# Last batch of a fused cross-attention kernel: value columns ahead of residual additions, copies ahead of the root, two scores moved, small operations later

## The chip, the cores and the metric

The kernel runs on one core of a Trainium2 chip. The time is that of one execution on the device, in microseconds (us). Five engines matter: TensorE (PE in the profile) for matrix products, VectorE (DVE), ScalarE (ACT) and GpSimd (POOL) for elementwise work, and SyncE (SP), whose queue issues the DMAs.

## The reference

Eight batches of 112 queries with 320 channels attend, with 20 heads of 16 channels, to 371 text tokens; four more tokens are image prompts. Beside the usual attention, the text probabilities also weight the raw 512-wide text embeddings; that weighted sum is normalised and compared with the normalised prompts, and the comparison is added to the prompts' own scores. Everything is float32.

```python
q = heads(hidden_states @ W_q)
k_t, v_t = heads(text_ehs @ W_k), heads(text_ehs @ W_v)
probs_t = softmax(einsum('bhsd,bhtd->bhst', q, k_t) * attn_scale)
text_out = einsum('bhst,bhtd->bhsd', probs_t, v_t)
attn_scores = einsum('bhsd,bhnd->bhsn', q, k_ip) * attn_scale      # four prompts
qsem = l2norm(einsum('bhst,bte->bhse', probs_t, text_ehs))
sem = einsum('bhsd,bnd->bhsn', qsem, l2norm(ip_ehs))
probs_ip = softmax(attn_scores + SEM_SCALE * sem) * spatial_mask
out = (text_out + einsum('bhsn,bhnd->bhsd', probs_ip, v_ip)) @ W_out + b_out + residual
```

## The kernel before

The batches 0 to 7 are worked through in turn, each in five groups g = 0 to 4 of four heads. The norm of the weighted embeddings is had without forming them: with p the unnormalised probabilities of a head and G the Gram matrix of the text tokens, p G is formed, and its dot product with p is the squared norm. So each head has, in `u`, the columns of G with 21 more columns beside them: four for the prompts, one of ones and sixteen for the head's values. One chain of products per head gives all of it in one bank `ps_qd` of 112 x 392.

A head passes through these helpers:

- `scores` (L652, TensorE): q k into a score bank `ps_s`, 375 columns with the prompts.
- `maxima` (L674, VectorE) and `exponentials` (L688 and L690, ScalarE): negated row maximum `nmx`, p = exp, and a copy `ipl` of the four prompt scores, which is the last reader of the score bank. `probabilities` is both, and `sent` (L695, SyncE) a DMA that deals p into `xg`.
- `turned` (L704, VectorE): the transposes of `xg` into `xgT`, in two halves.
- `multiplied` (L723, TensorE): twelve steps j, in each of which the four heads of the group run side by side in row groups of 32, from 392 columns at j = 0 down to 40. The helper yields after every step, and other work is put between the steps.
- `placed` (L621, GpSimd): copies the group's value columns from `vr` into `u`, in three chunks. The products of the group need them, and a chunk can be overwritten only when the group before has read it.
- `reduced` (L769, VectorE, `junk`): the dot product with p of one head. `shared` does the same for some heads with other engines: copies out of the bank on ScalarE (L753 value sums `pvs`, L754), a product on GpSimd (L758), a sum on ScalarE (L762). `value_sums` (L736) copies `pvs` for the heads that `shared` doesn't take.

`finish` then handles all heads of a batch: `z2`, `zr`, the division `attn` (L811, GpSimd), `rn` (L824), its root (L828, ScalarE, table Sqrt), a preload of the Exp table (L829), the reciprocal of `rn` and four more operations on `fu` (L834 to L840, VectorE), `ex` (L844, ScalarE), `sx`, `rx`, `w` (L848 to L852, VectorE), and then `ps_wT`, `wT`, `ps_a`, `aT`, `ps_o` (L858 to L894). It is a generator; each call of `run` or `next` issues one piece of it. `with_bias` (L783, GpSimd) adds bias to the residual. `last_heads` does the same for the last four heads of the last batch.

The order of instructions on every engine is written out by hand: the program text is the order. The steady loop `steps` covers batches 0 to 6. The last batch, b = 7, is a loop of its own at the end, in which the `finish` of batch 6 (`before`), the tail of batch 5 (its `ps_o` and output) and that of batch 7 itself (`first`, 16 heads, and `last`, 4 heads) are interleaved with the groups. There the scores of group 3 and group 4 are made in groups 0 and 1. Of the eight banks of 512 columns, four are `ps_qd`, two `ps_sc` and two `ps_mm`. `bank(..., spare=True)` takes a `ps_sc` bank, `bank(...)` a `ps_mm` bank. The scores of group 4 use the `ps_qd` banks, since groups 1 and 3 of the last batch accumulate in the other four.

Of the kernel before, what the change touches and what calls it, by code (L numbers as in the profile page):

```python
# [9 lines left out]
AF = mybir.ActivationFunctionType  # L10
# [10 lines left out]
def kernel(  # L21
# [63 lines left out]
    def bank(name, spare=False):  # L85

        if spare:
            return ps_sc.tile([P, 512], F32, tag="sc", name=name)
        return ps_mm.tile([P, 512], F32, tag="mm", name=name)
# [602 lines left out]
    def sent(b, g, a):  # L692

        xg = x_ring[(b * NG + g) % NX]
        nc.sync.dma_start(xg[a * RG : a * RG + S // QN, :, :TT], st[b]["p", g][:, a, :])  # L695
# [69 lines left out]
    def reduced(b, g, a0=0, a1=GROUP):  # L765
        s = st[b]
        for a, (h, ps) in list(enumerate(zip(groups[g], s["qd", g])))[a0:a1]:
            junk = small.tile([S, TT], F32, tag="junk", name=f"junk_{b}_{h}", bufs=1)
            nc.vector.tensor_tensor_reduce(  # L769
                out=junk,  # L770
                in0=ps[:S, :TT],
                in1=s["p", g][:, a, :],
                scale=1.0,
                scalar=0.0,
                op0=ALU.mult,
                op1=ALU.add,
                accum_out=s["ss"][:, h : h + 1],
            )
        if a1 == GROUP:
            del s["p", g]  # L780
# [5 lines left out]
    def finish(b, heads=(0, H), bd=None):  # L786
# [20 lines left out]
        ah = attn[:, :C].rearrange("p (h d) -> p h d", d=D)[:, part]  # L807

        def divided():
            nc.vector.reciprocal(zr, z)  # L810
            eng.tensor_tensor(  # L811
                ah, pvs[:, :, NIP + 1 :], zr.unsqueeze(2).to_broadcast([S, n, D]), ALU.mult
            )
# [4 lines left out]
                with_bias(b)  # L818
        nc.vector.scalar_tensor_tensor(z2, z, EPS * EPS, z, ALU.mult, ALU.mult)
        if bd is not None:  # L820
            divided()
            yield

        nc.vector.tensor_tensor(rn, s["ss"][:, part], z2, ALU.max)  # L824
        if bd is None:
            yield
# [1 line left out]
        nc.scalar.activation(rn, rn, AF.Sqrt)  # L828
        nc.scalar.preload_act_table(AF.Exp)  # L829
        if bd is None:  # L830
            divided()
        yield

# [217 lines left out]
    def drain(*gens):  # L1051
        for gen in gens:
            for _ in gen:
                pass
# [5 lines left out]
    def run(key, make, pieces=1):  # L1060

        if key not in gens:
            gens[key] = make()
        for _ in range(pieces):
            next(gens[key], None)
# [141 lines left out]
    for n, (b, g) in enumerate(steps[:-NG]):  # L1207
        if n == len(steps) - NG - 3:
            ctx.enter_context(
                tc.manual_schedule(  # L1210
                    engines=engines | {mybir.EngineType.Activation, mybir.EngineType.Pool}
                )
            )
        now, more, then = ahead(n)
        for c, a in now:
            scores(*c, a)
            probabilities(*c, a)
        for j, _ in enumerate(multiplied(b, g)):
            if j == 0:
                for c, a in more:  # L1220
                    scores(*c, a, ps=bank(f"ps_s_{c[0]}_{c[1]}_{a}"))
                    probabilities(*c, a, hold=True)
            if j == 5:
                for c, a in then:
                    scores(*c, a)
                held = more + [(c, a) for c, a in then if c == steps[n + LEAD + 1]]
                for c, a in then:
                    probabilities(*c, a, hold=(c, a) in held)
                drain(turn)
                for c, a in held:  # L1230
                    sent(*c, a)
            if j == 2:
                if g == 0:
                    gram_banks(b + 1)
                turn = turned(*steps[n + 1], 2 * QN)
                next(turn)
                if n == 0:
                    run(("c", LEAD), None)
                if 1 <= g <= 3:
                    gram_to_groups(b + 1, {1: (0,), 2: (1,), 3: (3,)}[g], parts=halves[g == 2])  # L1240
                for c, i in x_loads.get((b, g), ())[:1]:
                    load_x_blocks(c, i)

                if g in (1, 2) and b > 0:
                    run(("f", b - 1), None)
        value_sums(b, g)
        if g == 2 and b > 0:
            run(("f", b - 1), None)
        if n == len(steps) - NG - 1:
            sums = shared(b, g, GROUP // 2)  # L1250
            next(sums)
            reduced(b, g, 2)
        else:
            reduced(b, g)
        placed(*steps[n + 1])
        if g == 0 and b > 1:
            run(("f", b - 2), None)
        load_rest(n)
        if n == 0:
            load_embed(nc.sync, wkip_sb, w_k_ip)  # L1260
            load_embed(nc.sync, wvip_sb, w_v_ip)
        if g in ctx_blocks and b < B - 3:
            load_ctx_blocks(b + 3, ctx_blocks[g])
        for c, i in x_loads.get((b, g), ())[1:]:
            load_x_blocks(c, i)
        if g == 1:
            gram_to_groups(b + 1, (0,), parts=halves[1])
            gram_to_groups(b + 1, (1,), parts=halves[0])
        elif g == 2:
            gram_to_groups(b + 1, (2,))  # L1270
        elif g == 3:
            gram_to_groups(b + 1, (3,), parts=halves[1])
        if g in (2, 3) and b == 0:
            run(("pp",), None)
        if (b, g) == (B - 2, 0):
            prompt_values_by_head()
        if (b, g) == (B - 2, 1):
            bd = load_prompt_values_by_head()
        if (b, g) == (B - 2, 3):
            own_channels(bd)  # L1280
        if g == 0 and b > 0:
            prompt_values(b - 1)
        between(b, g)
        if n == NG - 1:
            drain(prompt_logits(b))
# [1 line left out]

    b = B - 1
    before = ("f", b - 1)
    next(sums)  # L1290
    run(("q", b), None)

    for g in range(NG):
        for j, _ in enumerate(multiplied(b, g)):
            if g == 0 and j in (0, 3):
                some = (2, 3) if j == 0 else (0, 1)
                for a in some:
                    scores(b, NG - 2, a, ps=bank(f"ps_s_{b}_{NG - 2}_{a}", spare=a > 1))
                for a in some:
                    probabilities(b, NG - 2, a, hold=True)  # L1300
                if j == 0:
                    turn = turned(b, 1)
                    next(turn)
                else:
                    drain(turn, sums)
                    for a in (2, 3, 0, 1):
                        sent(b, NG - 2, a)
            if g == 1 and j in (5, 6):
                for a in ((3, 2), (1, 0))[j - 5]:
                    ps = ps_qd.tile([P, 512], F32, tag="qd", name=f"ps_s_{b}_{NG - 1}_{a}")  # L1310
                    scores(b, NG - 1, a, ps=ps)
                    probabilities(b, NG - 1, a, hold=True)
                if j == 6:
                    drain(turn)
                    for a in (3, 2, 1, 0):
                        sent(b, NG - 1, a)
                    nc.scalar.preload_act_table(AF.Sqrt)
                    run(before, None)
            if (g, j) in ((2, QN), (2, 2 * QN), (3, QN)):
                run(before, None)  # L1320
            if g > 1 and j == 2 * QN:
                drain(sums)
            if 0 < g < NG - 1 and j in (QN - 1, 2 * QN - 1):
                placed(b, g + 1, (j // QN,))
        if g == NG - 1:
            break
        n = (3, 3, 2, 1)[g]
        earlier, sums = sums, shared(b, g, n)
        next(sums)
        reduced(b, g, n)  # L1330
        if g < NG - 2:
            value_sums(b, g, n)
            turn = turned(b, g + 2)
            if g == 0:
                next(turn)
            else:
                drain(turn, earlier)
            placed(b, g + 1, range(NT) if g == 0 else (NT - 1,))
            next(sums)
        if g == 0:  # L1340
            run(before, lambda: finish(b - 1, bd=bd[:, 0]))
            with_bias(b - 1)
            with_bias(b)
            run(("f", b - 2), None)
        if g == 2:
            nc.scalar.preload_act_table(AF.Sqrt)
        if g == 3:
            value_sums(b, g, 1)
            placed(b, g + 1, (NT - 1,))
            drain(sums)  # L1350
            first = finish(b, (0, FULL * HC), bd=bd[:, 1])
            for _ in range(4):
                next(first)
    late = projected_prompts(bd[:, 1])
    last = last_heads(b)
    run(before, None)
# [68 lines left out]
```

## Time and profile before

| | |
|---|---|
| median of three runs (lowest, highest) | 408.5 us (407.34, 408.51) |
| profiled execution, its own time | 407.31 us |
| span of its instructions | 405.6 us |
| granted TensorE clock | 0.999 |
| TensorE busy | 398.2 us, 98% of the span |
| VectorE, ScalarE, GpSimd busy | 341.1, 190.6, 118.2 us |

The own time of the profiled execution lies 1.7 us above its span. It is as short as the lowest of the three runs. In the rows of a timeline the columns are start and length in us, engine, line, operation, the tile written and the tiles read, shapes, and the number of instructions that the row merges; in brackets stands the idle time of the engine ahead of it and what ended it. The last batch takes from about 363 us to the end.

### The profile page before, as it was taken

Reading aid. Unit: us, or ns where it says so; the run is one execution under the profiler, and the core shown is the slowest. Engines: PE = TensorE matmul, PEld = TensorE weight load, DVE = VectorE, ACT = ScalarE, POOL = GpSimd, SP = SyncE. Lnnn points to the kernel's source line nnn. Section 1 sums busy time; section 2 is a strip of 40 time slices with the busy share of each in tenths; the row PEclk is TensorE's granted clock in tenths of the full one; section 3 lists DMA queues with packets and bytes.
Section 4 is the critical chain, followed back from the end, with each engine's and each line's share of the span. In section 5 each row is a group of like instructions: output and inputs, shape, how many; then the busy total and the mean of one; then the engine's idle time right before and its main releaser. Section 6 shows DMA issues by size and latency. Waiting matters only on the chain.

```text
span 405.6 us, 13896 instructions
## 1 busy us (share of the span) xinstructions
PE 398.2 (98%) x5442; PEld 313.9 (77%) x5442; DVE 341.1 (84%) x730; ACT 190.6 (47%) x664; POOL 118.2 (29%) x282
## 2 busy tenths in 40 slices
PE   9999999999999999999999999999999999999796
PEld 8658787987788877787777877788778887788793
DVE  5678797888998899788998989789898878886985
ACT  3553343545335634446334453445434463455883
POOL 6611110111342206022061212512143220715640
PEclk9999999999999999999999999999999999999999
DMA  6984665656645555465555555454445355544400
GB/s 214 215 186 115 218 165 146 155 153 183 151 126 135 159 146 141 106 152 168 138 146 145 149 145 137 118 141 149 121 118 142 99 172 140 134 113 127 116 3 30
DMA packets 46433, 56.94 MB, mean 140 GB/s; under 512 B 9405, under 2 KB 40961, under 8 KB 46368
## 3 DMA queue, kind: packets, MB, share of 16 engines
q1 hardware_dynamic: 46328, 55.99, 52.2%
q8 instruction: 43, 0.70, 0.7%
q14 instruction: 22, 0.18, 0.1%
q10 hardware_dynamic: 40, 0.07, 0.1%
HBM read 15.88 MB, written 1.39 MB: 43 GB/s over the span
## 4 chain that ended last, share of the span: by engine, by line
PE 95%; POOL 1%; issue 1%; ACT 1%; DVE 1%; POOLq 0%; DVEq 0%
PE ps_qd L723 40%; PE ps_k L541 16%; PE ps_s L652 11%; PE ps_v L541 10%; PE ps_g L507 7%; PE ps_q L359 4%; PE ps_o L943 3%; PE ps_g L463 1%; POOL shared L758 1%; PE ps_w L442 1%; PE ps_o L894 1%; PE ps_c L426 0%; PE ps_a L931 0%; PE ps_ipkv L298 0%; DVE nmx L674 0%
## 5 line engine op out<-in xcount | busy, mean ns | idle before, releaser
L723 PE MATMUL ps_qd<-u,xgT 32*112 32x168 f32 (+11 forms) x3840 | 216.6, 350 | 2.8 <-POOL u L621 2.8
L723 PEld LDWEIGHTS ps_qd<-u,xgT 32*112 32x112 f32 x3840 | 185.7, 172 | 27.3 <-POOL u L621 3.0
L688 ACT ACTIVATE p<-ps_s,nmx 112x371 f32<-112x371 f32 x156 | 84.3, 578 | 96.0 <-DVE nmx L674 89.5
L704 DVE STREAM_TRANSPOSE xgT<-xg 128x512 f32<-128x512 f32 (+2 forms) x79 | 126.0, 1598 | 0.7 <-DMA xr_sb<-in_x_dram 0.4
L674 DVE TENSOR_REDUCE nmx<-ps_s 112x1 f32<-112x371 f32 x160 | 78.8, 537 | 26.9 <-PE ps_s L652 22.7
L769 DVE CUSTOM_DVE_ANT_0 junk<-ps_qd,p 112x371 f32<-112x371 f32 x146 | 79.2, 542 | 19.5 <-ACT pvs L736 3.9
L621 POOL COPY u<-vr 128x64 f32<-128x64 f32 x120 | 26.4, 239 | 140.5 <-PE ps_qd L723 96.5
L652 PE MATMUL ps_s<-kT,qm 32*112 32x375 f32 (+1 forms) x320 | 64.7, 495 | 0.0
L541 PE MATMUL ps_k<-ctxT,wk_sb 128*128 128x371 f32 x192 | 64.6, 484 | 0.0
L541 PEld LDWEIGHTS ps_k<-ctxT,wk_sb 128*128 128x128 f32 x192 | 35.1, 190 | 20.3 <-ACT vT L563 0.5
L541 PE MATMUL ps_v<-ctxT,wv_sb 128*128 128x371 f32 x128 | 42.4, 482 | 0.0
L541 PEld LDWEIGHTS ps_v<-ctxT,wv_sb 128*128 128x128 f32 x128 | 23.7, 190 | 14.5 <-issue 0.5
L652 PEld LDWEIGHTS ps_s<-kT,qm 32*112 32x112 f32 x320 | 25.0, 171 | 12.6 <-issue 10.8
L507 PE MATMUL ps_g<-ctxT 128*32 128x375 f32 (+11 forms) x672 | 30.4, 333 | 0.0
L507 PEld LDWEIGHTS ps_g<-ctxT 128*32 128x32 f32 x672 | 27.7, 110 | 2.0
L556 ACT COPY kT<-ps_k 128x371 f32<-128x371 f32 x24 | 11.2, 468 | 37.9 <-PE ps_k L541 37.9
L690 ACT COPY ipl<-ps_s 112x4 f32<-112x4 f32 x140 | 23.0, 164 | 0.0
L414 DVE STREAM_TRANSPOSE ctxT<-ct 128x512 f32<-128x512 f32 x21 | 22.8, 1095 | 0.0
L918 POOL TENSOR_TENSOR wv<-vip,w 112x1280 f32<-112x1280 f32 x6 | 14.8, 2464 | 26.5 <-DVE w L852 26.5
L479 ACT ACTIVATE ug<-ps_g 128x375 f32<-128x375 f32 (+2 forms) x24 | 8.3, 375 | 24.5 <-issue 11.1
L563 ACT COPY vT<-ps_v 128x371 f32<-128x371 f32 x16 | 7.5, 468 | 25.5 <-PE ps_v L541 25.5
L480 POOL TENSOR_TENSOR ug<-ug,half 128x128 f32<-128x128 f32 (+1 forms) x24 | 10.4, 447 | 28.1 <-ACT ug L479 28.1
(164 smaller groups left out, 320.9 us busy)
## 6 DMA issues: line engine op xcount, KB each, us to landing
xg<-p SPq DMA_DIRECT2D x156, 162.3 KB
u<-ug SPq DMA_DIRECT2D x122, 99.0 KB
ct<-in_ctx_dram SPq DMA_DIRECT2D x28, 176.0 KB
vip<-vipd SPq DMA_DIRECT2D x6, 560.0 KB
xr_sb<-in_x_dram SPq DMA_DIRECT2D x32, 35.0 KB
out_dram<-ob SPq DMA_DIRECT2D x8, 140.0 KB
x_sb<-in_x_dram SPq DMA_DIRECT2D x6, 140.0 KB
xg<-wv_sb SPq DMA_DIRECT2D x4, 162.3 KB
```

What stands on the lines that cost most here:

```text
L359: nc.tensor.matmul(ps[:, : n * S], wq_sb[:, j, i * P : (i + 1) * P], xT[:, j, :n, :, : S // QN], start=(j == 0), stop=(j == NC - 1),)
L414: nc.vector.transpose(ctxT[:, :, c * P : (c + 1) * P].rearrange("p e (j i) -> p j e i", i=RG), ct[:, some, :].rearrange("p j (k e) -> p j ...
L507: nc.tensor.matmul(ps[c][q * RG : (q + 1) * RG, j * RG - c * P : T - c * P], ctxT[:, e, j * RG : (j + 1) * RG], ctxT[:, e, j * RG : T], st ...
L541: nc.tensor.matmul(ps[:, :TT], w[:, e, i * P : (i + 1) * P], ctxT[:, e, :TT], start=(e == 0), stop=(e == NE - 1),)
L621: nc.gpsimd.tensor_copy(v, dealt(b, c, s["vr"][:, c * QN : (c + 1) * QN, min(g + g // NE, 2 * NC - 1), :]))
L652: nc.tensor.matmul(ps[:S, :w], qm[a * RG : (a + 1) * RG, i, r, j * S : (j + 1) * S], s["kT"][a * RG : (a + 1) * RG, i, :w], start=True, st ...
L674: nc.vector.tensor_reduce(nmx, s["sc", g, a][:S, :TT], AX.X, ALU.max, negate=True)
L688: nc.scalar.activation(s["p", g][:, a, :], ps[:S, :TT], AF.Exp, bias=nmx)
L690: nc.scalar.copy(s["ipl"][:, groups[g][a], :], ps[:S, TT:T])
L704: nc.vector.transpose(xT[:, j0:j1].rearrange("p j (k q) -> p q j k", q=QN), xg[:, :, j0 * RG : j1 * RG].rearrange("p q (j k) -> p q j k", ...
L723: nc.tensor.matmul(banks[a][:S, j * RG : UW], xT[a * RG : (a + 1) * RG, j, :S], region(b, c)[a * RG : (a + 1) * RG, q, j * RG - c * P :], ...
L769: nc.vector.tensor_tensor_reduce(out=junk, in0=ps[:S, :TT], in1=s["p", g][:, a, :], scale=1.0, scalar=0.0, op0=ALU.mult, op1=ALU.add, accu ...
```

## The change

Only the order of instructions at the end of the program changes; the work is the same. At the end of batch 6 (group 4), GpSimd's two products of `shared` go ahead of `placed` for the last batch, and the scores and probabilities of two heads of group 3 go right behind that group's products, ahead of `ps_o` and `ps_q`. In group 0 of the last batch the other two scores take `ps_mm` banks at j = 1, and the transposes of group 1 follow them. In group 1 the scores of group 4 come one step earlier, with the sums of group 0 ahead of their exponentials. The pieces of batch 6's `finish` move: its first piece now ends ahead of the division, the division and both residual additions come behind the value columns for group 2, the Sqrt table, the root and the Exp table behind group 1's copies, the reciprocal and `fu` behind the transposes of group 4, `ex` and another Sqrt table ahead of group 3's copies, and `sx`, `rx`, `w` into the middle of batch 7's `first`.

```diff
@@ -807,7 +807,6 @@
         ah = attn[:, :C].rearrange("p (h d) -> p h d", d=D)[:, part]
 
         def divided():
-            nc.vector.reciprocal(zr, z)
             eng.tensor_tensor(
                 ah, pvs[:, :, NIP + 1 :], zr.unsqueeze(2).to_broadcast([S, n, D]), ALU.mult
             )
@@ -818,9 +817,10 @@
                 with_bias(b)
         nc.vector.scalar_tensor_tensor(z2, z, EPS * EPS, z, ALU.mult, ALU.mult)
         if bd is not None:
+            nc.vector.reciprocal(zr, z)
+            yield
+
             divided()
-            yield
-
         nc.vector.tensor_tensor(rn, s["ss"][:, part], z2, ALU.max)
         if bd is None:
             yield
@@ -828,6 +828,7 @@
         nc.scalar.activation(rn, rn, AF.Sqrt)
         nc.scalar.preload_act_table(AF.Exp)
         if bd is None:
+            nc.vector.reciprocal(zr, z)
             divided()
         yield
 
@@ -1250,6 +1251,10 @@
             sums = shared(b, g, GROUP // 2)
             next(sums)
             reduced(b, g, 2)
+            next(sums)
+            for a in (2, 3):
+                scores(B - 1, NG - 2, a)
+                probabilities(B - 1, NG - 2, a, hold=True)
         else:
             reduced(b, g)
         placed(*steps[n + 1])
@@ -1287,39 +1292,33 @@
 
     b = B - 1
     before = ("f", b - 1)
-    next(sums)
     run(("q", b), None)
 
     for g in range(NG):
         for j, _ in enumerate(multiplied(b, g)):
-            if g == 0 and j in (0, 3):
-                some = (2, 3) if j == 0 else (0, 1)
-                for a in some:
-                    scores(b, NG - 2, a, ps=bank(f"ps_s_{b}_{NG - 2}_{a}", spare=a > 1))
-                for a in some:
+            if g == 0 and j == 1:
+                drain(sums)
+                for a in (0, 1):
+                    scores(b, NG - 2, a, ps=bank(f"ps_s_{b}_{NG - 2}_{a}"))
                     probabilities(b, NG - 2, a, hold=True)
-                if j == 0:
-                    turn = turned(b, 1)
-                    next(turn)
-                else:
-                    drain(turn, sums)
-                    for a in (2, 3, 0, 1):
-                        sent(b, NG - 2, a)
-            if g == 1 and j in (5, 6):
-                for a in ((3, 2), (1, 0))[j - 5]:
+                drain(turned(b, 1))
+                for a in (2, 3, 0, 1):
+                    sent(b, NG - 2, a)
+            if g == 1 and j in (4, 5):
+                if j == 4:
+                    drain(sums)
+                for a in ((3, 2), (1, 0))[j - 4]:
                     ps = ps_qd.tile([P, 512], F32, tag="qd", name=f"ps_s_{b}_{NG - 1}_{a}")
                     scores(b, NG - 1, a, ps=ps)
                     probabilities(b, NG - 1, a, hold=True)
-                if j == 6:
+                if j == 5:
                     drain(turn)
                     for a in (3, 2, 1, 0):
                         sent(b, NG - 1, a)
-                    nc.scalar.preload_act_table(AF.Sqrt)
-                    run(before, None)
-            if (g, j) in ((2, QN), (2, 2 * QN), (3, QN)):
+            if (g, j) == (3, 2 * QN):
+                drain(sums)
                 run(before, None)
-            if g > 1 and j == 2 * QN:
-                drain(sums)
+                nc.scalar.preload_act_table(AF.Sqrt)
             if 0 < g < NG - 1 and j in (QN - 1, 2 * QN - 1):
                 placed(b, g + 1, (j // QN,))
         if g == NG - 1:
@@ -1333,24 +1332,32 @@
             turn = turned(b, g + 2)
             if g == 0:
                 next(turn)
+                run(before, lambda: finish(b - 1, bd=bd[:, 0]))
             else:
-                drain(turn, earlier)
+                drain(turn)
             placed(b, g + 1, range(NT) if g == 0 else (NT - 1,))
+            if g == 1:
+                with_bias(b - 1)
+                with_bias(b)
             next(sums)
+            if g == 1:
+                nc.scalar.preload_act_table(AF.Sqrt)
+            elif g == 2:
+                drain(earlier)
+            if g > 0:
+                run(before, None)
         if g == 0:
-            run(before, lambda: finish(b - 1, bd=bd[:, 0]))
-            with_bias(b - 1)
-            with_bias(b)
             run(("f", b - 2), None)
-        if g == 2:
-            nc.scalar.preload_act_table(AF.Sqrt)
         if g == 3:
             value_sums(b, g, 1)
             placed(b, g + 1, (NT - 1,))
             drain(sums)
             first = finish(b, (0, FULL * HC), bd=bd[:, 1])
-            for _ in range(4):
-                next(first)
+            next(first)
+            next(first)
+            run(before, None)
+            next(first)
+            next(first)
     late = projected_prompts(bd[:, 1])
     last = last_heads(b)
     run(before, None)
```

How this moves instructions is seen in the order of three engines. In the names, the first number is the batch and the second the group (or, for `finish`, the first head).

On GpSimd, between the products for groups 0 and 1 of the last batch, before:

```order
L758 TENSOR_TENSOR shared_7_0_5325<-shared_7_0_5325,p_7_0_4977 112x371 x3
L811 TENSOR_TENSOR attn_0_153<-pvs_6_3352,zr_6_0_5345 112x320
L783 TENSOR_TENSOR xb_6_5346<-x_sb_82,bias_sb_92 112x320
L783 TENSOR_TENSOR bd_4816<-x_sb_82,bias_sb_92 112x320
L621 COPY u_7_4035<-vr_7_4036 128x4x16 x3
L758 TENSOR_TENSOR shared_7_1_5441<-shared_7_1_5441,p_7_1_5038 112x371 x3
L621 COPY u_7_4035<-vr_7_4036 128x4x16 x3
```

and now:

```order
L758 TENSOR_TENSOR shared_7_0_5325<-shared_7_0_5325,p_7_0_4977 112x371 x3
L621 COPY u_7_4035<-vr_7_4036 128x4x16 x3
L783 TENSOR_TENSOR xb_6_5340<-x_sb_82,bias_sb_92 112x320
L783 TENSOR_TENSOR bd_4816<-x_sb_82,bias_sb_92 112x320
L758 TENSOR_TENSOR shared_7_1_5437<-shared_7_1_5437,p_7_1_5038 112x371 x3
L810 TENSOR_TENSOR attn_0_153<-pvs_6_3352,zr_6_0_5339 112x320
L621 COPY u_7_4035<-vr_7_4036 128x4x16 x3
```

The value columns for group 2 (the first copies) have gone ahead of the division and the two residual additions (`bd` is reused as the seventh batch's `xb`), and the division behind the products of group 1.

On VectorE, from the transposes for group 4 of the last batch on, before:

```order
L704 STREAM_TRANSPOSE xgT_7_4_5538<-xg_1_152 128x4x192 x2
L848 TENSOR_REDUCE sx_6_0_5570<-ex_6_0_5510 112x20
L850 RECIPROCAL rx_6_0_5572<-sx_6_0_5570 112x20
L852 TENSOR_SCALAR w_6_0_5574<-ex_6_0_5510,sm_sb_91,rx_6_0_5572 112x80
L769 ISA junk_7_11_5610,ss_7_4038<-ps_qd_7_3_1_5546,wv_sb_86 112x371
```

and now:

```order
L704 STREAM_TRANSPOSE xgT_7_4_5526<-xg_1_152 128x4x192 x2
L835 RECIPROCAL rn_6_0_5338<-rn_6_0_5338 112x20
L837 TENSOR_TENSOR fu_6_0_5536<-pvs_6_3352,rn_6_0_5338 112x80
L838 TENSOR_SCALAR fu_6_0_5536<-fu_6_0_5536,ipl_6_3350 112x80
L840 TENSOR_REDUCE mx_6_0_5539<-fu_6_0_5536 112x20
L841 TENSOR_TENSOR fu_6_0_5536<-fu_6_0_5536,mx_6_0_5539 112x80
L769 ISA junk_7_11_5604,ss_7_4038<-ps_qd_7_3_1_5543,wv_sb_86 112x371
```

The five operations from the reciprocal to `fu` of batch 6, which stood ahead of the junk sums of group 2 and of these transposes, are now behind the transposes; `sx`, `rx` and `w` of batch 6 stand further behind, between `rn` and its reciprocal of batch 7.

On ScalarE, around the copies of group 3's first bank, before:

```order
L736 COPY pvs_7_4039<-ps_qd_7_2_3_5464 112x21
L1346 ACT_TABLE_LOAD
L762 ACTIVATE shared_7_2_5527,ss_7_4038<-shared_7_2_5527 112x371 x2
L753 COPY pvs_7_4039<-ps_qd_7_3_0_5545 112x21
L754 COPY shared_7_3_5607<-ps_qd_7_3_0_5545 112x371
```

and now:

```order
L762 ACTIVATE shared_7_1_5437,ss_7_4038<-shared_7_1_5437 112x371 x3
L762 ACTIVATE shared_7_2_5515,ss_7_4038<-shared_7_2_5515 112x371 x2
L845 ACTIVATE ex_6_0_5586<-fu_6_0_5536 112x80
L1321 ACT_TABLE_LOAD
L753 COPY pvs_7_4039<-ps_qd_7_3_0_5542 112x21
L754 COPY shared_7_3_5601<-ps_qd_7_3_0_5542 112x371
```

The exponential of batch 6 and the table load for the next root stand directly ahead of the copies of group 3, the load behind the exponential.

## The prediction

> **What bounds the kernel now.** I read the page's head and its chain first, then TensorE's waits, then the timelines of TensorE, GpSimd, ScalarE and VectorE over the last batch, since the change touches nothing before 362 us.
>
> ```profile
> span 405.6 us, 13896 instructions
> PE 95%; POOL 1%; issue 1%; ACT 1%; DVE 1%; POOLq 0%; DVEq 0%
> ...
> PE ps_qd L723 <- POOL u L621: 2.8, 2, 1.4
> ...
> 378.06 5.11 PE L723 MATMUL ps_qd<-u,xgT 32*112 32x392 f32 x96 [1.38 <-POOL u L621]
> 384.58 9.61 PE L723 MATMUL ps_qd<-u,xgT 32*112 32x392 f32 x192 [1.41 <-POOL u L621]
> 394.12 0.29 PE L858 MATMUL ps_wT<-ident,w 112*80 112x112 f32 x1
> 394.76 0.47 PE L878 MATMUL ps_a<-wT,bd 80*128 80x112 f32 x2
> ...
> 402.60 0.32 SPq L1046 DMA_DIRECT2D out_dram<-ob  x1
> ```
>
> TensorE carries 95% of the chain. It stands still twice in the last batch, ahead of groups 2 and 3, each time for GpSimd's value columns: 2.8 us in all. That is the most the change can win among the groups. Groups 3 and 4 together take 9.61, so 4.8 each. Behind them, from 394.12 on, comes a tail of small steps that ends with the output's DMA at 402.60; a gain among the groups counts only if this tail starts earlier as well.
>
> **The change part by part.** *Scores ahead of the root.* Two scores of group 3 now stand between the sixth batch's last products and ps_o.
>
> ```profile
> 363.16 1.87 PE L943 MATMUL ps_o<-wo_sb,aT 128*112 128x320 f32 x6
> 363.43 0.17 ACT L690 COPY ipl<-ps_s 112x4 f32<-112x4 f32 x1
> 363.74 0.91 ACT L754 COPY shared<-ps_qd 112x371 f32<-112x371 f32 x2
> 365.62 1.22 PE L723 MATMUL ps_qd<-u,xgT 32*112 32x392 f32 x10
> 366.38 0.48 PE L652 MATMUL ps_s<-kT,qm 32*112 32x375 f32 x2
> 366.39 1.91 POOL L758 TENSOR_TENSOR shared<-shared,p 112x371 f32<-112x371 f32 x2
> 366.69 0.48 PE L652 MATMUL ps_s<-kT,qm 32*112 32x375 f32 x2
> ```
>
> The second of them takes over the bank that the ipl copy releases at 363.43 + 0.17 = 363.60. A score has two passes, 0.31 apart (366.38, 366.69): 0.62, so ps_o begins at about 364.3 and not 363.16. ps_o and ps_q keep their 365.62 − 363.16 = 2.46, and group 0 begins at 366.7, 1.1 later. There the two scores no longer stand, which gives 0.62 back. Two products (1.91) also go ahead of group 0's value columns on GpSimd: its first copy comes after the ScalarE copies (364.3 for the first) + 1.9 + 0.24, so 366.5. Group 0 needs it at 366.7: hidden by 0.2, and any more comes on top. The other two scores take banks that ps_o and ps_q used; those are read by 367.5, the scores come at 368: hidden. The four sends of group 3 still follow its last probabilities, and the seventh batch's reciprocal of z, made one step earlier on VectorE, is of no length that matters.
>
> *Groups 0 and 1.*
>
> ```profile
> 371.26 3.57 PE L723 MATMUL ps_qd<-u,xgT 32*112 32x392 f32 x50
> 372.72 2.78 POOL L758 TENSOR_TENSOR shared<-shared,p 112x371 f32<-112x371 f32 x3 [1.19 <-ACT shared L754]
> 375.46 0.74 POOL L811 TENSOR_TENSOR attn<-pvs,zr 112x320 f32<-112x320 f32 x1
> 376.97 0.86 POOL L783 TENSOR_TENSOR bd<-x_sb,bias_sb 112x320 f32<-112x320 f32 x1
> 377.78 0.58 POOL L621 COPY u<-vr 128x64 f32<-128x64 f32 x3
> 377.90 0.21 ACT L690 COPY ipl<-ps_s 112x4 f32<-112x4 f32 x1
> ```
>
> Group 0 takes 4.8 + 0.62, so group 1 begins at 372.1 against 371.26: 0.8 late. Before, GpSimd's row reads products, division (attn), two residual additions, then the columns at 377.78, and TensorE started 0.28 behind them. Now the columns come ahead of the division and the additions; they wait only for TensorE's own reading of the region, to about 377.4. But group 2 needs four banks, and these hold the scores of group 4 until the last ipl copy, which ended at 377.90 + 0.21 = 378.11. The scores move one step earlier in group 1 (about 0.4) and group 1 is 0.8 later: the last bank is free at 378.5, and this releases group 2 and not the columns. The three sums (L762) now ahead of the Exp are covered, for the products end at 375.5 as before (other sums held the copies then, the later group 0 does now). So group 2 ends at 378.5 + 4.6 = 383.1, as before (378.06 + 5.11 = 383.17; its last row group had waited for the same bank). What goes as a wait for GpSimd comes back as a wait for ScalarE.
>
> *Group 3.*
>
> ```profile
> 378.13 1.28 ACT L1317 ACT_TABLE_LOAD   x1
> 379.42 0.22 ACT L828 ACTIVATE rn<-rn 112x20 f32<-112x20 f32 x1
> 381.58 2.75 POOL L758 TENSOR_TENSOR shared<-shared,p 112x371 f32<-112x371 f32 x3 [3.22 <-ACT shared L754]
> 384.28 0.60 POOL L621 COPY u<-vr 128x64 f32<-128x64 f32 x3
> ```
>
> Before, two table loads and a root (378.13 to 380.94) stood ahead of group 1's copies on ScalarE; so GpSimd's products began at 381.58 and the columns at 384.28. Now the copies go first (about 378.6), products from 379.3 to 382.0, the division 0.74 to 382.8, and then the columns, first one at 383.0. TensorE needs it at 383.1. Group 3 starts at 383.1 instead of 384.58, **−1.5**, and the products end at 392.6. Here the change does what its words say.
>
> *The tail.* It lies behind VectorE and ScalarE, where the later small operations now are.
>
> ```profile
> 378.77 3.53 SPq L695 DMA_DIRECT2D xg<-p  x4
> ...
> 381.85 0.25 DVE L834 RECIPROCAL rn<-rn 112x20 f32<-112x20 f32 x1
> 384.35 0.53 DVE L769 CUSTOM_DVE_ANT_0 junk<-ps_qd,p 112x371 f32<-112x371 f32 x1
> 385.51 3.02 DVE L704 STREAM_TRANSPOSE xgT<-xg 128x768 f32<-128x768 f32 x2
> 388.34 0.20 DVE L848 TENSOR_REDUCE sx<-ex 112x20 f32<-112x80 f32 x1
> 389.53 0.55 DVE L769 CUSTOM_DVE_ANT_0 junk<-ps_qd,wv_sb 112x371 f32<-112x371 f32 x1 [0.22 <-PE ps_qd L723]
> 392.22 0.17 DVE L824 TENSOR_TENSOR rn<-ss,z 112x16 f32<-112x16 f32 x1
> 392.68 0.25 DVE L834 RECIPROCAL rn<-rn 112x16 f32<-112x16 f32 x1 [0.28 <-ACT rn L828]
> 393.74 0.22 DVE L840 TENSOR_TENSOR fu<-fu,mx 112x64 f32<-112x64 f32 x1
> ...
> 387.32 1.28 ACT L1346 ACT_TABLE_LOAD   x1
> 389.68 0.47 ACT L754 COPY shared<-ps_qd 112x371 f32<-112x371 f32 x1
> 391.58 0.52 ACT L762 ACTIVATE shared<-shared 112x371 f32<-112x371 f32 x1
> 393.99 0.26 ACT L844 ACTIVATE ex<-fu 112x64 f32<-112x64 f32 x1
> 394.45 0.25 ACT L864 COPY wT<-ps_wT 80x112 f32<-80x112 f32 x1 [0.20 <-PE ps_wT L858]
> ...
> 390.22 0.97 POOL L758 TENSOR_TENSOR shared<-shared,wv_sb 112x371 f32<-112x371 f32 x1 [0.25 <-ACT shared L754]
> ```
>
> After group 2, VectorE makes two junk sums (384.35 to 385.51: 1.16), now from 383.4 to 384.6, then the two transposes for group 4 (385.51 to 388.34: 2.83) to 387.4. These need their DMAs: 3.53, issued near 379.1, landed by 382.7, covered by 1.9; if that cover goes, the lateness adds to all below. Only then come the five fu operations of the sixth batch, which before ran at 381.85 ahead of the junk sums. Their like in the seventh takes 392.68 to 393.96 = 1.28; the sixth's own took 381.85 to 384.35 = 2.50, beside GpSimd's products of 381.58. So fu ends at 388.7 or 389.9. ScalarE's ex (0.26) follows, then the table load that the change puts behind it (1.28): 390.4 or 391.6. Only then can group 3's copy run, which stood at 389.68 with its load already done at 387.32. I take the short price for the chain and a quarter of the difference (1.22 / 4 = 0.3), because GpSimd there runs only single value copies, nearer to the row at 392.68 than to that at 381.85.
>
> From the copy at 390.45 on: GpSimd starts 0.54 behind it and needs 0.97, so the sum L762 is at 392.0 (391.58 before, where three junk sums also held it), rn at 392.65 (392.22). Then sx, rx and w of the sixth batch (388.34 to 389.31 = 0.97) stand ahead of the seventh's reciprocal; the root on ScalarE hides 392.68 − 392.22 = 0.46 of it. The reciprocal comes at 393.65: **+0.97**. fu and ex of the seventh follow unchanged, so ex is at 394.95. The sixth's wT copy stands behind that ex on ScalarE, as before, and moves from 394.45 to 395.4; the products L878 go from 394.76 to 395.7. TensorE, done with its groups at 392.6, waits. All behind hangs on these steps: the tail ends 0.95 later, and the 1.5 of group 3 is lost in full.
>
> [...]
>
> [...]
>
> The sum: 0.95 + 0.3 = **+1.3 us**. Against the profiled execution's own 407.31 (span 405.6) that is 408.6 (406.9). This execution is as short as the lowest of the three runs, 407.34, and 1.2 under their median 408.5; against the median, **409.8**. The likeliest case's own range is +0.5 (half of the 0.95 turns out to be hidden) to +2.2 (0.95 + 1.22): 409.0 to 410.7.
>
> **The rivals.** *The tail follows the products.* The gain at group 3 goes through if group 3's copy runs right behind its products, at 389.68 − 1.5 = 388.2; for this the table load must begin by 386.9. The sum above has it at 389.1. It turns if fu needn't wait for the transposes, or ScalarE's load isn't held by ex. For it: the rows at 389.53 (released by TensorE's products) and 394.12 show that before the tail did follow the products. Against it: what stands ahead of the load is in fixed order and has 2.83 + 1.28 + 0.26 to do after 384.6. Price −1.0 (w of the sixth still ahead of the reciprocal, 0.97 − 0.46) to −1.5: 407.0 to 407.5. This is the side of faster.
>
> *The front costs more.* Group 0's columns are ready only 0.2 ahead, the bank at 378.5 hangs on ScalarE's order, and the fu operations could meet GpSimd fully: +2.2 to +3.0, 410.7 to 411.5. For it: these covers are small, and the tail's chain starts at group 2's end, so nothing behind hides them. Against it: group 2 waited for the same bank before and ended at 383.17 all the same.
>
> *It balances.* The tail's junk sums and copies come earlier than I think, and half of the 1.5 survives: −0.3 to +0.9, 408.2 to 409.4. For it: three junk sums now run from 388.7 and not 389.53.
>
> **How the numbers follow.** About 0.3% (1.2 us) is what a measurement of this kernel can tell from no change. The forecast's case (+0.5 to +2.2) has 0.62, of which 0.42 lie above 1.2 and 0.20 below. The costly front 0.10, all slower. The balance 0.13, nearly all same. The gain 0.15, all faster but for 0.01, and the balance gives 0.02 more. Faster 0.16, same 0.32, slower 0.52. The range: 407.3 to 411.0 leaves out some two thirds of the gain (0.10) and most of the costly front (0.06), under 2 in 10.
>
> **What would show it right or wrong.** Right: TensorE's ps_o near 364.3, group 2 released by the ipl copy near 378.5 and not by GpSimd, group 3 at 383.1 without a gap, new gaps of TensorE near 393 and 394.5 behind VectorE's w and ScalarE's wT copy; ScalarE's load at 389 ahead of group 3's copy at 390.4; the seventh's reciprocal at 393.65. Wrong: that copy at 388.2 (the gain is real), the columns of group 3 after 383.5, or the clock below full in the new gaps.

## The result and the profile after

The changed kernel takes 411.67 us (median of ten executions, 410.25 to 413.52) against 407.93 for the kernel before in the same ten rounds. The ratio is 1.0095, with a 95% interval of 1.0074 to 1.0115: 3.9 us slower (3.0 to 4.7). The forecast was 409.8 with a range to 411.0, so the sign was right and the size was not. The profiled execution took 413.52, at the upper end.

The page, with the granted clock in its last two slices, TensorE's waits, and the waits' place in the timeline:

```profile
span 411.8 us, 13894 instructions
...
PEclk9999999999999999999999999999999999999976
...
PE ps_wT L859 <- DVE w L853: 1.7, 1, 1.7
PE ps_a L879 <- ACT wT L865: 0.9, 1, 0.9
...
365.35 1.87 PE L944 MATMUL ps_o<-wo_sb,aT 128*112 128x320 f32 x6
376.61 17.20 PE L723 MATMUL ps_qd<-u,xgT 32*112 32x232 f32 x338
395.46 0.27 PE L859 MATMUL ps_wT<-ident,w 112*80 112x112 f32 x1 [1.66 <-DVE w L853]
397.05 0.77 PE L879 MATMUL ps_a<-wT,bd 80*128 80x112 f32 x2 [0.86 <-ACT wT L865]
401.80 5.09 PE L895 MATMUL ps_o<-wo_sb,aT 128*112 128x320 f32 x10
```

The two waits for GpSimd's value columns (2.8 us) are gone; from 376.61 TensorE works without a pause through the groups, to 393.81. In their place stand two waits of the tail, 1.7 for the sixth batch's w and 0.9 for its wT copy. And something else shows that no wait lists: the ten passes of ps_o at 401.80 take 5.09. In the kernel before the same ten take

```profile
397.72 2.87 PE L894 MATMUL ps_o<-wo_sb,aT 128*112 128x320 f32 x10
```

The busy time and granted clock of TensorE by stretch say why. First the kernel after, then before; the columns are the stretch, its length, the busy time of TensorE, its weight loads, VectorE, ScalarE and GpSimd with instruction counts, the granted clock, and the DMA's share and rate.

```profile
392.65:396.06 3.41, 1.75 (x46) 1.48 (x38) 2.70 (x10) 2.13 (x5) 1.67 (x3) 1.00 0.00 0
396.06:406.30 10.24, 9.38 (x28) 6.09 (x28) 5.64 (x26) 4.32 (x14) 0.72 (x3) 0.50 0.00 1
```

```profile
391.40:394.80 3.40, 3.40 (x79) 3.16 (x71) 2.22 (x12) 2.78 (x9) 0.86 (x2) 1.00 0.02 5
394.80:402.60 7.80, 7.07 (x34) 4.05 (x33) 5.81 (x24) 4.14 (x12) 0.73 (x3) 1.00 0.06 18
```

After a stretch of 3.41 us in which TensorE was busy for only 1.75, the clock is 0.50 for 10.24 us, through nearly the whole tail. Before, it stays at 1.00 to the last product. The ten executions bear it out: the two with the highest mean clock (0.996) took 410.25 and 410.33, the two with the lowest (0.985) 413.43 and 413.52.

The steps of the sum are to be seen in the other engines' rows; the last line is a piece of the chain that ended last:

```profile
362.76 0.99 DVE L674 TENSOR_REDUCE nmx<-ps_s 112x1 f32<-112x371 f32 x2
378.43 1.58 DVE L704 STREAM_TRANSPOSE xgT<-xg 128x768 f32<-128x768 f32 x1
384.19 0.55 DVE L769 CUSTOM_DVE_ANT_0 junk<-ps_qd,p 112x371 f32<-112x371 f32 x1 [0.86 <-PE ps_qd L723]
386.09 3.04 DVE L704 STREAM_TRANSPOSE xgT<-xg 128x768 f32<-128x768 f32 x2 [0.65 <-DMA xg<-p]
388.98 0.22 DVE L835 RECIPROCAL rn<-rn 112x20 f32<-112x20 f32 x1
390.06 0.24 DVE L841 TENSOR_TENSOR fu<-fu,mx 112x80 f32<-112x80 f32 x1
395.23 0.24 DVE L835 RECIPROCAL rn<-rn 112x16 f32<-112x16 f32 x1
...
379.18 0.21 ACT L690 COPY ipl<-ps_s 112x4 f32<-112x4 f32 x1
390.62 1.28 ACT L1321 ACT_TABLE_LOAD   x1
391.99 0.47 ACT L754 COPY shared<-ps_qd 112x371 f32<-112x371 f32 x1
396.76 0.23 ACT L865 COPY wT<-ps_wT 80x112 f32<-80x112 f32 x1
...
383.91 0.68 POOL L621 COPY u<-vr 128x64 f32<-128x64 f32 x3
...
380.07 3.56 SPq L695 DMA_DIRECT2D xg<-p  x4
...
382.83 3.13 DMA xg<-p
```

The row at 362.76 is the last one ahead of the change; in the kernel before it stands here:

```profile
361.88 0.99 DVE L674 TENSOR_REDUCE nmx<-ps_s 112x1 f32<-112x371 f32 x2
```

So this execution was already 0.88 late when the changed part began, from parts that the change doesn't touch. All comparisons of its rows with the forecast take that off.

### The profile page after: what moved, and what is told of

Its sections match the earlier page's. It is cut to its first block, busy times and chain, and to the rows that moved or that the text cites. A ratio compares the mean times of both kernels' runs of the same rounds, so it can differ in the third digit from the quotient of the medians.

```text
span 411.8 us, 13894 instructions
## 1 busy us (share of the span) xinstructions
PE 404.9 (98%) x5442; PEld 317.7 (77%) x5442; DVE 339.5 (82%) x730; ACT 190.5 (46%) x664; POOL 118.2 (29%) x282
## 4 chain that ended last, share of the span: by engine, by line
PE 94%; DVE 2%; DMA 2%; ACT 1%; issue 0%; POOL 0%; DVEq 0%; POOLq 0%; ACTq 0%
PE ps_qd L723 38%; PE ps_k L541 15%; PE ps_s L652 11%; PE ps_v L541 10%; PE ps_g L507 7%; PE ps_q L359 4%; PE ps_o L944 3%; PE ps_g L463 2%; PE ps_o L895 1%; DVE xgT L704 1%; DMA xg<-p 1%; DMA xg<-wv_sb 1%; PE ps_w L442 1%; PE ps_a L879 1%; PE ps_c L426 0%
## 5 line engine op out<-in xcount | busy, mean ns | idle before, releaser
L723 PE MATMUL ps_qd<-u,xgT 32*112 32x328 f32 (+11 forms) x3840 | 217.0, 350 | 0.0
```

The source lines that it names most:

```text
L723: nc.tensor.matmul(banks[a][:S, j * RG : UW], xT[a * RG : (a + 1) * RG, j, :S], region(b, c)[a * RG : (a + 1) * RG, q, j * RG - c * P :], ...
```

## The experiments

Extra products, where there are any, are these, written into columns of a bank that nobody reads:

```python
def idle(o, n):
    one = nc.const_aps.tensor(1.0, [P, o.shape[1]], F32)
    for _ in range(n):
        nc.tensor.matmul(o, one[:, :P], one, start=True, stop=True)
```

**The clock alone: e1_tensor_fill.**

```diff
             ps = bank(f"ps_wT_{b}")
+            if h1 == H:
+                idle(ps[:, 2 * P : 2 * P + 200], 3)
...
             ps = bank(f"ps_a_{b}_{h0}", spare=n < H)
+            if h1 == H:
+                idle(ps[:, NC * S : NC * S + 176], 2)
```

> The changed kernel with five extra matrix products of constants on TensorE in its two new idle stretches (three of 200 columns ahead of the sixth batch's transpose of w, two of 176 ahead of the transposes into ps_a); their results are never read. Theory: the small operations reach the tail about 1.4 us late, and the rest of the loss (some 2.2 us in the median, 3.9 in the profiled execution) is TensorE's clock, which falls to half because of these idle stretches. Then the granted clock stays at 1.0 to the end and the time is about 1.4 above before, 409.3, with little spread. Rival: the clock is a symptom of the runs and not of the stretches, the whole loss is the order of the instructions: then the time stays at 411.7.

Measured, near the expectation: 409.51 us, all six executions within 408.81 to 409.74 and with a clock of 0.998 or more; ratio to before 1.0043 (1.0029 to 1.0056), so +1.75 us. Its stretches (here and below the helper's line numbers move by a few):

```profile
393.30:396.70 3.40, 2.88 (x23) 2.12 (x18) 2.35 (x11) 2.43 (x8) 0.81 (x2) 1.00 0.00 0
396.70:404.80 8.10, 7.03 (x33) 4.07 (x33) 6.14 (x26) 4.15 (x12) 0.72 (x3) 1.00 0.05 15
...
400.02 2.87 PE L905 MATMUL ps_o<-wo_sb,aT 128*112 128x320 f32 x10
```

The stretch that was half idle is now busy for 2.88 of 3.40, the clock stays at 1.00, and ps_o takes 2.87 again. Kernel e1 does more work than the changed one and is, by the ratios, 2.1 us faster. The loss thus has two parts: 1.75 is the order of the instructions, 2.1 is the clock.

**A pause in the kernel before: e6_pause_before and e6f_pause_filled.** To see whether idle time alone does it, the kernel before gets two more table loads ahead of the seventh batch's exponential; the second kernel fills the pause with seven products.

```diff
         nc.scalar.preload_act_table(AF.Exp)
+        if h1 < H:
+            nc.scalar.preload_act_table(AF.Sqrt)
+            nc.scalar.preload_act_table(AF.Exp)
```

> The kernel before, unchanged but for two more table loads on ScalarE between the seventh batch's root and its exponential (2 x 1.28 us). TensorE then stands idle for some 2.5 us ahead of the products into ps_a. Theory: a single idle stretch of this size makes the granted clock fall to half for one or more stretches of 3.4 us behind it: clock 0.985 to 0.996, time 2.4 to 2.6 above before from the loads and 1 to 3 more from the clock, 411 to 413, with a spread of over 2 us. Rival (the clock's fall belongs to the order of the changed kernel, not to idle time): clock 0.998 or more, 410.0 with a spread under 2 us.

> e6_pause_before with seven products of 176 columns in that idle stretch, results unread. Theory: clock 0.998 or more, time 2.4 to 2.6 above before, 410.0, and the difference to e6_pause_before is the price of the clock, 1 to 3 us. Rival: the same as e6_pause_before.

Measured: 412.39 (ratio 1.0110, 1.0094 to 1.0125; clock 0.989 to 0.992 in all four) and 410.40 (1.0060, 1.0046 to 1.0073; clock 0.998 to 1.000 in all six). The stretches of the paused kernel, then of the filled one:

```profile
395.70:399.10 3.40, 1.30 (x10) 1.08 (x11) 1.22 (x5) 2.38 (x9) 0.43 (x2) 1.00 0.00 0
399.10:405.97 6.87, 6.87 (x18) 4.20 (x17) 4.03 (x19) 3.57 (x6) 0.29 (x1) 0.50 0.00 1
```

```profile
394.40:397.80 3.40, 3.40 (x24) 3.06 (x25) 0.67 (x3) 3.03 (x9) 0.20 (x1) 1.00 0.00 0
397.80:405.00 7.20, 6.46 (x30) 3.43 (x28) 5.33 (x24) 3.81 (x7) 0.53 (x2) 1.00 0.03 9
```

One pause of 2.10 ahead of the products into ps_a, no reordering, and the clock falls to 0.50 for 6.87 us; filled, it stays at 1.00. The pause itself costs 2.4, about what its two loads of 1.28 make; the clock adds 2.0. The expected spread of over 2 us did not show in the four executions of the paused kernel (412.06 to 413.14).

**What in the order costs: e2, e8, e3, e10.** In e2 the sixth batch's reciprocal and fu go back ahead of group 2's junk sums; e8 is e2 with two filling products.

```diff
             break
+        if g == 2:
+            run(before, None)
         n = (3, 3, 2, 1)[g]
...
-            if g > 0:
+            if g == 1:
                 run(before, None)
```

> The changed kernel with the sixth batch's reciprocal and four fu operations back ahead of group 2's junk sums on VectorE (the rest of the change stays). In the trace VectorE then stands idle or waits for a DMA, so the transposes for group 4 should not start later. Theory: the table load ahead of group 3's copies comes about 1.9 us earlier, w is ready before TensorE's products end, TensorE's first stretch vanishes and the second shrinks to some 0.7; the clock stays at 1.0; time 0.4 under before, 407.5. Rival (the transposes and their DMA set the tail, or the front does): the time stays above before by 1 us or more.

> e2_fu_ahead with two extra products of 176 columns ahead of the transposes into ps_a, results unread. The four executions of e2_fu_ahead with a clock of 0.999 took 407.8 to 408.1, 0.3 to 0.5 above the before of that call. Theory: with the clock held, the five operations behind the transposes for group 4 are most of what the order costs: 0.3 to 0.5 above before, against 1.75 for e1_tensor_fill. Rival (fu only moves the loss, the table load or sx, rx, w hold the tail as well): 1.0 or more above before.

Measured: e2 408.75, ratio 1.0029 (1.0014 to 1.0044), 1.2 above before and not 0.4 under. The expectation of the clock was wrong: a wait of 0.9 for the wT copy was left, and in eight of twelve executions the clock fell (0.996 or less, 408.4 to 410.7); the four at 0.999 took 407.8 to 408.1. With the wait filled, e8: 407.86, ratio 0.9994 (0.9982 to 1.0006), even less than the 0.3 to 0.5 above before that was expected. The five operations behind the transposes thus cost 2.0 us (1.0043 against 0.9994, uncertain by about 0.75, an estimate from the two intervals). From the maxima at the start of the changed part to the end of the span, one execution each, it is less: 407.8 − 362.51 = 45.29 in e1 and 407.2 − 363.25 = 43.95 in e8, a difference of 1.3. In e8 the five fill time in which VectorE of the changed kernel waits (0.86 ahead of the junk sum, 0.65 ahead of the transposes), and the transposes start hardly later (386.63 − 363.25 = 23.38 behind the maxima, in the changed kernel 386.09 − 362.76 = 23.33), with their data there:

```profile
363.25 0.99 DVE L680 TENSOR_REDUCE nmx<-ps_s 112x1 f32<-112x371 f32 x2
384.14 0.28 DVE L841 RECIPROCAL rn<-rn 112x20 f32<-112x20 f32 x1 [0.29 <-ACT rn L834]
386.63 3.05 DVE L710 STREAM_TRANSPOSE xgT<-xg 128x768 f32<-128x768 f32 x2
```

In e3 the two scores go back into group 0; in e10 the `next(sums)` ahead of `placed` goes back behind it as well, so that GpSimd's two products follow the value columns, and TensorE's stretches are filled as in e1. The scores' edit:

```diff
-            for a in (2, 3):
-                scores(B - 1, NG - 2, a)
-                probabilities(B - 1, NG - 2, a, hold=True)
...
+            if g == 0 and j == 0:
+                for a in (2, 3):
+                    scores(b, NG - 2, a, ps=bank(f"ps_s_{b}_{NG - 2}_{a}", spare=True))
+                    probabilities(b, NG - 2, a, hold=True)
```

> The changed kernel with the two scores of group 3 back in group 0 at j = 0, as before, and all else as changed. Theory: ps_o comes 1.2 us earlier, the groups end about 0.5 earlier, but the tail's chain over the transposes for group 4 is only moved by as much, so the idle stretches and the half clock stay: time 0.4 to 0.6 under the changed kernel, 411.1. Rival (the front carries the loss): down to 409 or less.

> e1_tensor_fill with the front as before the change (two scores in group 0 at j = 0, GpSimd's two products behind the value columns). Theory: the front costs what e5 and e7 differ by, about 1.0, because the tail's chain starts at group 2's end: 0.6 to 1.0 above before. Rival (the DMAs for group 4's transposes or ScalarE hold the chain, not the front): 1.75 above before as e1.

Measured: e3 411.79, ratio 1.0101 (1.0073 to 1.0130), no gain where 0.4 to 0.6 was expected, and its page shows what ate it:

```profile
L723 PE MATMUL ps_qd<-u,xgT 32*112 32x104 f32 (+11 forms) x3840 | 217.2, 350 | 0.8 <-POOL u L621 0.8
```

With ps_o early, group 0 waits 0.8 us for its value columns, which still stand behind GpSimd's two products. This experiment alone, with the clock falling in it too (0.985 to 0.996), would have acquitted the front. With both parts undone and the stretches filled, e10: 408.34, ratio 1.0011 (0.9997 to 1.0024), 1.3 us under e1; 0.4 above before, where 0.6 to 1.0 was expected, and one of its twelve executions still fell to 0.996. From the maxima to the end of the span, one execution each, it is 406.4 − 362.01 = 44.39, 0.9 under e1. The front does cost. Two timelines, e1 first, then e10:

```profile
362.51 1.00 DVE L680 TENSOR_REDUCE nmx<-ps_s 112x1 f32<-112x371 f32 x2
365.10 1.87 PE L954 MATMUL ps_o<-wo_sb,aT 128*112 128x320 f32 x6
393.49 1.29 PE L448 MATMUL ps_wT<-const-float32-1.0 128*128 128x200 f32 x6
```

```profile
362.01 1.00 DVE L680 TENSOR_REDUCE nmx<-ps_s 112x1 f32<-112x371 f32 x2
363.30 1.87 PE L954 MATMUL ps_o<-wo_sb,aT 128*112 128x320 f32 x6
391.82 1.29 PE L448 MATMUL ps_wT<-const-float32-1.0 128*128 128x200 f32 x6
```

From the maxima to ps_o it is 2.59 in e1 and 1.29 in e10: the scores put ps_o 1.3 late. From ps_o to the end of the groups it is 28.39 and 28.52: the pair that no longer stands in group 0 gives back 0.13.

**A better order: e4, e5, e7, e9.** Kernel e4 has fu ahead as e2, the sixth batch's ex and the Sqrt table behind group 2's copies, the sums of groups 1 and 2 behind those, and sx, rx, w behind group 3's junk sums.

```diff
-            if (g, j) == (3, 2 * QN):
-                drain(sums)
-                run(before, None)
-                nc.scalar.preload_act_table(AF.Sqrt)
...
             elif g == 2:
+                run(before, None)
+                nc.scalar.preload_act_table(AF.Sqrt)
                 drain(earlier)
...
             value_sums(b, g, 1)
+            drain(earlier)
             placed(b, g + 1, (NT - 1,))
             drain(sums)
+            run(before, None)
             first = finish(b, (0, FULL * HC), bd=bd[:, 1])
```

> The changed kernel with fu ahead of group 2's junk sums, ex and the table load directly behind group 2's copies, group 2's sums behind group 3's copies, and sx, rx and w of the sixth batch behind group 3's junk sums. Theory: the 1.2 to 1.5 us gained at group 3 now reach the tail: seventh batch's reciprocal 0.7 earlier than before, no idle stretch over 0.5 on TensorE, clock 1.0: time 0.7 to 1.2 under before, 406.7 to 407.2. Rival (the order of the small operations is not what holds the tail): at or above before.

> The kernel e4_tail_order with two extra products of 176 columns on TensorE, ahead of the transposes into ps_a, results unread. In e4 the executions with a mean granted clock of 0.998 or more took 406.9 to 408.1, those with 0.996 took 408.2 to 409.0. Theory: the idle stretch of 0.6 is enough to make the clock fall in some executions; filled, all executions have the clock of 0.998 or more and the median comes to 407.2, 0.3 to 0.8 under before. Rival: the clock follows the small size of the tail's products and not the idle stretch: some executions still fall to 0.996 and the median stays at 407.9.

> e5_order_and_fill with the front as before the change: GpSimd's two products behind the value columns for the last batch, and the two scores in group 0 at j = 0. Theory: the two scores ahead of ps_o cost 0.5 net at the start of group 1, and with GpSimd's columns first nothing else waits: 0.3 to 0.6 under e5, about 406.8. Rival (the change's front is free, since group 2 waits for its last bank anyway): the same as e5 within 0.2.

> e7_front_and_order without its two extra products. Theory: the idle stretch ahead of L879 is then some 0.6 as in e4_tail_order, and about half of the executions fall to 0.996 or lower: median 0.3 to 0.6 above e7, ratio to before 0.997 to 0.999. Rival (the filling does nothing here): the same ratio as e7, 0.9967.

Measured, as ratios to before: e4 1.0005 (0.9992 to 1.0018), e5 0.9991 (0.9981 to 1.0001), e7 0.9967 (0.9955 to 0.9979), e9 0.9980 (0.9958 to 1.0002). The gain expected of e4 is not there; e5 gains 0.4 where 0.3 to 0.8 was expected, not told from none; e7 gains 1.0 over e5, more than the 0.3 to 0.6 expected; e9 came out as expected. In e4 a wait of 0.6 for the wT copy is left:

```profile
394.05 0.47 PE L879 MATMUL ps_a<-wT,bd 80*128 80x112 f32 x2 [0.58 <-ACT wT L865]
...
393.00:396.38 3.38, 2.80 (x20) 1.89 (x20) 2.55 (x11) 2.31 (x11) 0.43 (x2) 1.00 0.00 0
396.38:399.78 3.40, 3.10 (x9) 1.94 (x9) 2.17 (x12) 2.57 (x4) 0.29 (x1) 0.50 0.01 2
```

The clock of this profiled execution is 0.50 for one stretch of 3.40 behind it; five of the twelve executions have a mean clock of 0.996. Filled (e5), the clock is at least 0.997 in all twelve, though the interval of the ratio still reaches 1. With the front undone as well, e7 is the fastest: 406.57 us median, 1.35 under before. Without its two filling products (e9) the executions fall into two halves: six with 0.999 or more took 405.8 to 406.2, six with 0.989 to 0.996 took 407.5 to 409.8. The two products cost about half a microsecond and leave one of ten executions at 0.996.

## Why the prediction was right or wrong, by its steps

*Group 3 and the columns*: right. Group 2's products end where the junk sum begins, 384.19 − 0.88 = 383.3 (forecast 383.4); TensorE goes on without waiting for GpSimd; the first of the value columns for group 3 starts at 383.91 − 0.88 = 383.0 (forecast 383.0); the groups end at 393.81 − 0.88 = 392.9 (forecast 392.6). What the change is built for is there.

*The front*: half right. ps_o at 365.35 − 0.88 = 364.5 (forecast 364.3). But the pair taken out of group 0 was priced at 0.62, its length, and gave back next to nothing: 0.13 in the timelines of e1 and e10. In the changed kernel the last products of group 0 release GpSimd's copy at 373.48 − 0.88 = 372.6, before at 371.29, so they are as late as ps_o, 1.3. Before, the pair had run beside products of the other row groups (the rows 365.62 and 366.38 overlap). So group 1 could begin only 1.3 late and not 0.8; but the scores of group 4 came only 0.4 late (375.78 − 0.88 = 374.9, before 374.51), so the step earlier was worth 0.9 and not 0.4. The last bank was free at 379.18 + 0.21 − 0.88 = 378.5, as forecast, because two errors cancel: that hit is luck. The prediction took the front as paid, since group 2 ended "as before". That was true, but without the front's 1.3 the groups end 1.2 earlier (29.81 behind the maxima in e10, 30.98 in e1) and the kernel 0.9 to 1.3.

*The transposes for group 4*: the cover was wrong. The row of 3.53 is the time in which the queue issues four DMAs, about 0.8 each (0.80 to 0.84 in the changed kernel), not the time in which they land. The issuing was forecast well: it begins at 380.07 − 0.88 = 379.2 (forecast 379.1), right behind the transposes of group 2 (378.43 + 1.58 = 380.01). The last DMA is issued at 382.83 and has landed 3.13 later, at 385.96; the transposes wait until 386.09, 0.65 of it idle. The prediction had "landed by 382.7, covered by 1.9". So the tail's chain runs through these DMAs and not only from group 2's end.

*fu, the table load, the copy*: the short price was right. 388.98 to 390.30 is 1.32 (forecast 1.28), so the quarter of the difference to 2.50 wasn't needed; a value copy of GpSimd stood beside them (389.35) and each of the five still took 0.22 to 0.24. The prediction's own terms up to the copy add up to 390.25, and its 390.4 holds some 0.2 that it doesn't name; from the reciprocal at 388.98 to the copy at 391.99 it took 3.01 where the terms make 2.82, so that 0.2 was there. The load follows ex, the copy stands at 391.99 − 0.88 = 391.1 (forecast 390.45, and 0.65 of DMA wait makes 391.1). The seventh batch's reciprocal: 395.23 − 0.88 = 394.35 against 393.65, late by the same 0.7. L879: 396.17 against 395.7. The load cost its own 1.28 here: begun at 390.62, it ends at 391.90, and the next copies on ScalarE begin at 391.92 and, the larger of them, at 391.99.

*The sum of the order*: inside its range, in part by luck. Forecast +1.3 with +0.5 to +2.2; measured with the clock held +1.75 (1.2 to 2.3). The sum held 0.3 for a part of the 2.50 that fu took before, where it took 1.32, and nothing for the DMAs, which took 0.65: with these two put right it is 0.95 + 0.65 = 1.6. By the ratios its parts are 2.0 for the small operations (e8), 1.3 for the front (e10), and what remains, 1.75 − 2.0 − 1.3 = −1.55, for the columns and copies, close to the −1.5 of the prediction. But that the parts add up is assumed, not measured, and each is uncertain by about 0.75. From the maxima to the end, one execution each, they are 1.34 and 0.90 out of 45.29 − 43.72 = 1.57 (before: 405.6 − 361.88), which leaves −0.67. How much of the −1.5 the kernel kept is not settled.

*The step that failed* is "TensorE, done with its groups at 392.6, waits", where the clock had no price. The sum worked out both new idle stretches and took them as idle time only; the half clock was named among the things that would prove the forecast wrong, without a chance or a cost, and the range ended at 411.0 for it. The price is 2.1 us in the median, by e1, and 3.75 in the profiled execution, the slowest (from the maxima to the end 411.8 − 362.76 = 49.04, in e1 45.29). The prediction gives no reason for leaving it out. Before, TensorE stood still for 1.38 and 1.41 with the clock at 1.00. But those pauses were followed by 5.11 and 9.61 us of dense products; the new ones, 1.66 and 0.86, lie between 393.81 and 397.05, with the fall at 396.06 between them, and are followed by the tail's small ones. That this makes the difference is argued; what the runs show is that a pause ahead of the tail was followed by the half clock (e6: 2.10, then 0.50 for 6.87 us) and that with the pauses filled the mean clock stayed at 0.998 or more (e1, e6f).

None of the rivals came about as told: the gain was there among the groups and lost behind them, and neither the columns nor the bank of group 2 held group 2 or 3 longer than forecast.

## What to carry to other kernels

When work is moved off the path, look at what TensorE does in the time it gains: if it stands idle ahead of a last serial chain, it may run that chain at half clock, as here (0.50 for 10.24 us). A few products of constants with unread results were a cheap test and nearly a cure (e7 and e10 had one execution each at 0.996 left). The length of the queue's row for a DMA was here the issuing (3.56 for four), so take the landing from who waits for it. And an experiment that undoes half a change can meet a new wait from the other half (e3), so undo both halves, with the clock held, before a part is acquitted.

## What the hardware showed that was not expected

The half-clock stretches of the profiled executions have lengths of 3.40 (e4), 6.82 (e2: 396.34 to 403.16), 6.87 (e6) and 10.24 us (the changed kernel): close to one, two and three times the shortest. Executions of one kernel differ by up to 4 us with their mean clock (e9: 405.82 at 0.999, 409.77 at 0.989). What sets these lengths, and in which executions the clock falls, no run shows.

The longest single pause ahead of the fall was 1.66 us in the changed kernel and 0.58 in e4. How far the busy time of TensorE ahead of it decides the fall isn't settled by these runs: in e4's profiled execution the clock fell behind 2.80 busy of 3.38, in e1's it did not behind 2.88 of 3.40 (a stretch whose ends the author chose), and the busy time of the tail's small products is modelled. The busy time also cannot be all that counts. In the kernel before, the stretch with the pause of 1.38 is

```profile
374.70:378.10 3.40, 2.02 (x56) 1.87 (x48) 2.76 (x5) 2.18 (x8) 3.40 (x6) 1.00 0.60 176
```

It is busy for 2.02, less than in e4, and the clock stays at 1.00 behind it. It has 56 products from several row groups, where e4's stretch has 20 of the tail's small ones. Whether the pause or the thin products around it bring the clock down is therefore open: the filling products take away both. Nor is the kernel before quite free of it: one of 73 later executions had a clock of 0.993 and took 410.18.
